# The block products of an f32 attention kernel as four products of 32 output rows, in column tiles

## The chip, the cores and the metric

One core of a Trainium2 chip. TensorE multiplies matrices and writes its results to PSUM (eight banks of 128 partitions by 512 f32 numbers); VectorE, ScalarE and GpSimd (POOL in the profile) read, add and copy; SyncE (SP) issues most of the DMAs between SBUF and memory. Each engine works through its own instructions in order, and engines wait for one another through semaphores. The metric is the time of one execution on the device, in microseconds (us).

## The reference

An input `x` of 8 batches, 512 positions and 512 features goes through attention with 16 heads of 32 features, whose queries and keys are conditioned by one vector a batch, and the result is added to `x`. All is float32. Without the reshaping into heads:

```python
Q, K, V = x @ Wq.T + bq, x @ Wk.T + bk, x @ Wv.T + bv
cQ = Q + (cond @ Wq.T + bq)
cK = K + (cond @ Wk.T + bk)
scores = cQ @ cK.T / sqrt(32)          # per batch and head
out = x + softmax(scores) @ V
```

## The kernel before, in words

Four heads make a group of 128 features, so there are 32 pairs of a batch and a head group, numbered `t` (`T = B * G`). The main loop goes over `t`, and each turn has four stages, `kc` from 0 to 3. In each stage TensorE does three things one after the other.

First come the scores of group `t` for 128 keys (`exponentials`, lines 565 to 584). Four matmuls with three rows each (L570, bf16) put the negated maxima of the queries into four PSUM banks, and four matmuls with 32 rows each (L573) add the scores. ScalarE turns the four banks into exponentials (L584).

Second come the row scores of group `t + 1` or `t + 2`, for 128 queries (`row_max`, `row_scores`, L499). They are used only for the maxima and the denominators: VectorE takes the maximum of each row (L490 for two banks, L508 for the other two together), and ScalarE takes the exponentials against it and adds them up (`denominators`, L518; each is followed by an instruction that reads the sum).

Third comes one of two things. In one stage of four it is the weighted sum of the group before (`weighted`, `times_v`, L589): four heads side by side, each with 32 columns of weights and its own 32 of the 128 output partitions, with 512 columns moving, and between them the sums' spreading (`spread_sums`, L620). VectorE then turns the result (L645), GpSimd divides and adds the residual (L646, L647), and SP stores it. In the other three stages it is a part of the projections of the next batch to queries, keys and values.

A projection of a pair of head groups is not computed as eight products of blocks but as seven, after Strassen and Winograd. The sums and differences of blocks of the weights (`combine_w`) and of the turned input (`combine_x`) are made ahead, and `product` (lines 397 to 406) multiplies one block by one block: 256 features are summed in two matmuls of 128 rows (`kc`), with 128 columns of weights held still and 256 columns moving, into half a bank. For queries and keys the block of the weights is still and the block of the input moves (L406); for the values it is the other way round (L403). `first_products` and `other_products` call it, seven matmuls' worth in each stage: the first does products 1, 6, half of 2, and 7; the other does 4, 5, the other half of 2, and 3. ScalarE copies product 1 away (L438), and VectorE adds the others up (L444 and L445 or L458 and L459, and `plus`, L426 or L429), reading the banks. The halves of a product are in the same order for every stage.

The order of all instructions on TensorE, ScalarE, VectorE and GpSimd is written out by hand (`tc.manual_schedule`). Which of the eight banks a stage uses for what is in the table `TURNS`, of which `banks` reads a row; the same pattern returns after two groups, that is eight stages. The maxima are split in three bf16 parts (`split_max`) and, in the main loop, turned by a DMA (`turn_max`), not by TensorE.

In the profile an f32 matmul of the program shows as two records on TensorE, each a weight load (engine PEld) and a pass (PE); a bf16 matmul shows as one. A stage with block products has 14 such records on lines 403 or 406.

Of the kernel before, what the change touches and what calls it, by code (L numbers as in the profile page):

```python
# [17 lines left out]
def kernel(  # L18
# [38 lines left out]
    nc = tc.nc  # L57
    P = 128
    B, S, D = x.shape
    HD = 32  # L60
    H = D // HD
    G = D // P
    HG = P // HD
# [5 lines left out]
    HS = S // 2  # L69
# [175 lines left out]
    for i in range(NS):  # L245
        r = slice(i * BL, (i + 1) * BL)
# [130 lines left out]
    def block_of_w(n, i, u, kc):  # L377
        f = MADE_OF[i - 1][0]
        if n == "v":
            at = slice(0, HS) if f != "22" else slice(HS, D)  # L380
            if isinstance(f, int):
                return wc[n][:, f, kc, :]
        else:
            g = u * 2 + (f == "22")
            at = slice(g * P, (g + 1) * P)
            if isinstance(f, int):
                return wc[n][:, f, kc, u * P : (u + 1) * P]
        return wT[n][:, kc + 2 * (f != "11"), at]

    def block_of_x(b, i, kc, at):  # L390
        f = MADE_OF[i - 1][1]
        if isinstance(f, int):
            return xc[:, f, kc, at]
        off = HS * (f == "22")
        return xT[b][:, kc + 2 * (f != "11"), at.start + off : at.stop + off]

    def product(n, b, u, i, pt, kcs=(0, 1)):

        for kc in kcs:
            w = block_of_w(n, i, u, kc)  # L400
            if n == "v":
                xb = block_of_x(b, i, kc, slice(u * P, (u + 1) * P))
                nc.tensor.matmul(pt, xb, w, start=(kc == kcs[0]), stop=(kc == kcs[-1]))  # L403
            else:
                xb = block_of_x(b, i, kc, slice(0, HS))
                nc.tensor.matmul(pt, w, xb, start=(kc == kcs[0]), stop=(kc == kcs[-1]))  # L406

    def twice(a):
        return a.unsqueeze(1).broadcast_to([P, 2, HS])
# [21 lines left out]
    def first_products(n, b, u, dens, small, at, first=0):  # L431


        one_, two_ = banks(first), banks(at)
        c1, c12, c2, c22 = parts_of(n, b, u)
        m1 = c2[:, 0, :]
        product(n, b, u, 1, one_[:, :HS])
        nc.scalar.copy(m1, one_[:, :HS])  # L438
        dens()
        product(n, b, u, 6, two_[:, :HS])  # L440
        small()
        product(n, b, u, 2, two_[:, HS:], (0,))
        product(n, b, u, 7, one_[:, HS:])
        nc.vector.tensor_tensor(c12, two_[:, :HS], m1, ALU.add)  # L444
        nc.vector.tensor_tensor(c1[:, 0, :], two_[:, HS:], m1, ALU.add)  # L445
        plus(n, b, u, 1, c22, one_[:, HS:], c12)
# [359 lines left out]
    for t in range(T - 3):  # L806
        b, r = divmod(t, G)
# [199 lines left out]
    b, g = divmod(t, G)  # L1007
# [55 lines left out]
```

## Time and profile before

| What | Value |
|---|---|
| median of 3 runs | 722.1 us (721.99 to 722.43) |
| the profiled execution | 722.59 us, of which the span is 720.8 us |
| TensorE passes busy | 714.2 us, 99% |
| TensorE weight loads busy | 401.3 us, 56% |
| VectorE busy | 528.0 us, 73% |
| ScalarE busy | 617.3 us, 86% |
| GpSimd busy | 176.3 us, 24% |
| DMA | 32.91 MB, mean 46 GB/s |

The span runs from the first instruction of the program to the last; the time of the execution has a little more around it. Busy time is the union of an engine's instructions, without the waits. Weight loads (PEld) overlap the passes (PE). In a row of a group or a chain, `L406` is line 406 of the kernel, `128*128 128x256` says that weights of 128 rows and 128 columns are held still and 256 columns move past 128 rows, and `x14` counts records. A row of busy times by stage has the stretch in us, its length, and then busy us and records of PE, PEld, VectorE (DVE), ScalarE (ACT) and POOL, the granted share of the TensorE clock, the DMA engines' mean busy share and the GB/s. In square brackets after a record stands how long its engine had been idle and what ended that. Where the text below gives start times with three decimals, they are those of single records of the trace, from the span's start.

### The profile page before, as it was taken

What the parts mean: (1) busy time and instruction counts of PE and PEld (TensorE: products, weight loads), DVE (VectorE), ACT (ScalarE), POOL (GpSimd) and SP (SyncE); (2) the same over time, 40 slices, a digit from 0 to 9 for tenths busy, and PEclk for the clock granted to TensorE, in tenths of its full rate; (3) what the DMA queues carried; (4) which work ended last, traced back from release to release, by engine and by line L of the source; (5) the groups of instructions that cost most, each with busy time, mean ns of one, the idle gap of its engine ahead of it and who ended that gap; (6) DMA issues with size and microseconds to landing.
All of it is one profiled execution on the core that took longest, in us unless ns stands there. A gap on an engine that the chain in (4) does not pass through costs nothing.

```text
span 720.8 us, 14892 instructions
## 1 busy us (share of the span) xinstructions
PE 714.2 (99%) x5296; PEld 401.3 (56%) x5296; DVE 528.0 (73%) x834; ACT 617.3 (86%) x1539; POOL 176.3 (24%) x275
## 2 busy tenths in 40 slices
PE   9999999999999999999999999999999999999997
PEld 7566555565555566555565555565555565555532
DVE  4798777777768777677776877777767767767777
ACT  2589989999899998989999889998989989889674
POOL 3712221122221122221122221122221122221351
PEclk9999999999999999999999999999999999999999
DMA  6733321222322222321322321323201222211211
GB/s 177 110 60 62 53 41 30 49 44 46 53 35 36 50 41 49 53 41 28 51 41 49 52 40 27 53 37 52 38 16 23 38 38 38 37 21 19 37 32 29
DMA packets 223358, 32.91 MB, mean 46 GB/s; under 512 B 221610, under 2 KB 222122, under 8 KB 223284
## 3 DMA queue, kind: packets, MB, share of 16 engines
q1 hardware_dynamic: 221524, 30.92, 25.3%
q10 hardware_dynamic: 1760, 1.05, 0.5%
q8 instruction: 41, 0.67, 0.4%
q14 instruction: 33, 0.27, 0.1%
HBM read 19.75 MB, written 8.39 MB: 39 GB/s over the span
## 4 chain that ended last, share of the span: by engine, by line
PE 97%; DVE 2%; issue 1%; DMA 1%; DVEq 0%
PE psum L406 27%; PE psum L499 16%; PE psum L589 15%; PE psum L403 14%; PE psum L573 14%; PE psum L570 5%; PE psum L350 2%; DVE acc L863 1%; PE psum L889 1%; DMA w_q<-in_L_cond_Wq_dram 1%; PE psum L266 0%; DVE acc L861 0%; PE psum L311 0%; PE psum L667 0%; PE psum L599 0%
## 5 line engine op out<-in xcount | busy, mean ns | idle before, releaser
L518 ACT ACTIVATE dead<-psum,nmax 128x512 f32<-128x512 f32 x480 | 327.6, 702 | 5.1 <-DVE nmax L490 3.1
L584 ACT ACTIVATE e<-psum 128x512 f32<-128x512 f32 x488 | 252.0, 602 | 64.2 <-PE psum L573 63.9
L490 DVE TENSOR_REDUCE nmax<-psum 128x1 f32<-128x512 f32 x240 | 154.5, 686 | 143.1 <-PE psum L499 143.1
L508 DVE TENSOR_REDUCE nmax<-psum 128x2 f32<-128x1024 f32 x130 | 157.7, 1214 | 2.8 <-PE psum L499 2.7
L499 PE MATMUL psum<-kT,qT 32*128 32x512 f32 x1024 | 143.9, 605 | 0.0
L646 POOL TENSOR_TENSOR res<-res,recs 128x512 f32<-128x512 f32 x30 | 31.5, 1049 | 432.1 <-DVE res L645 432.1
L573 PE MATMUL psum<-qT,kT 32*128 32x512 f32 x976 | 125.5, 587 | 0.0
L589 PE MATMUL psum<-e,v 128*32 128x512 f32 x1024 | 121.2, 596 | 0.0
L518 ACT ACTIVATION_READ_ACCUMULATOR dead<-psum,nmax 128x1 f32 x480 | 105.2, 219 | 0.0
L499 PEld LDWEIGHTS psum<-kT,qT 32*128 32x128 f32 x1024 | 59.8, 183 | 58.1 <-ACT dead L518 26.4
L589 PEld LDWEIGHTS psum<-e,v 128*32 128x32 f32 x1024 | 26.6, 110 | 65.1 <-issue 37.6
L573 PEld LDWEIGHTS psum<-qT,kT 32*128 32x128 f32 x976 | 48.6, 185 | 2.2
L403 PE MATMUL psum<-wc_v,xc 128*128 128x256 f32 x192 | 49.3, 379 | 0.0
L570 PE MATMUL psum<-maxT,onesb 3*128 3x512 bf16 x488 | 48.1, 384 | 0.0
L406 PE MATMUL psum<-xc,wc_k 128*128 128x256 f32 x180 | 46.2, 379 | 0.0
L406 PE MATMUL psum<-xc,wc_q 128*128 128x256 f32 x180 | 46.2, 379 | 0.0
L570 PEld LDWEIGHTS <-onesb 3*128 3x128 bf16 x488 | 12.3, 90 | 57.2 <-issue 57.2
L173 POOL TENSOR_TENSOR xr<-xr,bvs 128x512 f32<-128x512 f32 x31 | 39.4, 1272 | 18.7 <-DMA x<-in_x_dram 12.0
L403 PEld LDWEIGHTS psum<-wc_v,xc 128*128 128x128 f32 x192 | 36.5, 190 | 5.0
L647 POOL TENSOR_TENSOR res<-res,xr 128x512 f32<-128x512 f32 x30 | 38.2, 1273 | 2.4
L403 PE MATMUL psum<-wT_v,xT 128*128 128x256 f32 x128 | 37.1, 392 | 0.0
L406 PEld LDWEIGHTS psum<-xc,wc_k 128*128 128x128 f32 x180 | 34.2, 190 | 4.7
(165 smaller groups left out, 791.2 us busy)
## 6 DMA issues: line engine op xcount, KB each, us to landing
xr<-in_x_dram SPq DMA_DIRECT2D x124, 64.0 KB, 2.4
out_dram<-res SPq DMA_DIRECT2D x122, 64.0 KB, 1.9
x<-in_x_dram SPq DMA_DIRECT2D x112, 64.0 KB, 2.4
w_q<-in_L_cond_Wq_dram SPq DMA_DIRECT2D x4, 256.0 KB, 4.4
w_v<-in_L_cond_Wv_dram SPq DMA_DIRECT2D x16, 64.0 KB, 2.4
w_k<-in_L_cond_Wk_dram SPq DMA_DIRECT2D x16, 48.0 KB, 2.3
x<-in_x_dram ACTq DMA_DIRECT2D x2, 256.0 KB, 3.9
x<-in_x_dram SPq DMA_DIRECT2D x2, 256.0 KB, 4.2
```

What stands on the lines that cost most here:

```text
L173: nc.gpsimd.tensor_tensor(xr[t], xr[t], bias, ALU.add)
L403: nc.tensor.matmul(pt, xb, w, start=(kc == kcs[0]), stop=(kc == kcs[-1]))
L406: nc.tensor.matmul(pt, w, xb, start=(kc == kcs[0]), stop=(kc == kcs[-1]))
L490: nc.vector.tensor_reduce(nmax[t][:, qc, j : j + 1, 0], banks(HG + j), AX.X, ALU.max, negate=True)
L499: nc.tensor.matmul(pt, qkT["q", t][r, qc * P : (qc + 1) * P], qkT["k", t][r, :], start=True, stop=True,)
L508: nc.vector.tensor_reduce(nmax[t][:, qc, pr * 2 : pr * 2 + 2, 0], pt, AX.X, ALU.max, negate=True)
L518: nc.scalar.activation(dead, banks(HG + j), AF.Exp, bias=nmax[t][:, qc, j, :], accum_out=sums[t][:, qc, j, :],)
L570: nc.tensor.matmul(bank[j], onesb[r, :], maxT[t][r, :], start=True, stop=False)
L573: nc.tensor.matmul(bank[j], qkT["k", t][r, kc * P : (kc + 1) * P], qkT["q", t][r, :], start=False, stop=True,)
L584: nc.scalar.activation(e[:, i, :], bank[pr * 2 + i], AF.Exp)
L589: nc.tensor.matmul(pt[j * HD : (j + 1) * HD, :], vs[b % 2][:, kc, (g * HG + j) * HD : (g * HG + j + 1) * HD], es[t, kc, j // 2][:, j % 2, ...
L647: nc.gpsimd.tensor_tensor(y, y, xr.pop(t), ALU.add)
```

## The change

`product` splits every block matmul in four. Each of the four holds 32 of the 128 columns of the still block and writes the 32 output partitions that belong to them, in a column tile of its own; all four read the same moving block. This is the form that the weighted sum (L589) has, with 256 columns moving instead of 512. The two cases (values, queries and keys) now share one matmul line.

```diff
         for kc in kcs:
             w = block_of_w(n, i, u, kc)
             if n == "v":
-                xb = block_of_x(b, i, kc, slice(u * P, (u + 1) * P))
-                nc.tensor.matmul(pt, xb, w, start=(kc == kcs[0]), stop=(kc == kcs[-1]))
+                still, moving = block_of_x(b, i, kc, slice(u * P, (u + 1) * P)), w
             else:
-                xb = block_of_x(b, i, kc, slice(0, HS))
-                nc.tensor.matmul(pt, w, xb, start=(kc == kcs[0]), stop=(kc == kcs[-1]))
+                still, moving = w, block_of_x(b, i, kc, slice(0, HS))
+            for j in range(HG):
+                r = slice(j * HD, (j + 1) * HD)
+                nc.tensor.matmul(
+                    pt[r], still[:, r], moving, start=(kc == kcs[0]), stop=(kc == kcs[-1])
+                )
```

`HG` is 4 and `HD` is 32. Nothing else is changed: the blocks, the banks, the order of the stages and the work of the other engines are as before.

## The prediction

> **What bounds the kernel now.** The page's busy line, the clock row and the chain that ended last come first.
>
> ```profile
> PE 714.2 (99%) x5296; PEld 401.3 (56%) x5296; DVE 528.0 (73%) x834; ACT 617.3 (86%) x1539; POOL 176.3 (24%) x275
> PEclk9999999999999999999999999999999999999999
> ...
> PE 97%; DVE 2%; issue 1%; DMA 1%; DVEq 0%
> ```
>
> TensorE bounds nearly the whole span, at full clock. But ScalarE is busy 86%, so a gain on TensorE may soon meet it. The chain in order of time shows what a stage is made of (start, us, line, records):
>
> ```profile
> 305.39 0.33 PE psum L570 x4
> 305.71 0.86 PE psum L573 x8
> 306.57 0.94 PE psum L499 x8
> 307.51 3.22 PE psum L406 x14
> 310.73 0.33 PE psum L570 x4
> 311.06 0.86 PE psum L573 x8
> 311.92 0.86 PE psum L499 x8
> 312.78 0.99 PE psum L589 x8
> 313.77 0.05 PE psum L620 x7
> 313.82 2.59 PE psum L589 x24
> ```
>
> Every stage is exponentials' scores (L570, L573), row scores (L499), then either block products (L403/L406, seven products of two matmuls) or the weighted sum (L589). An f32 matmul is two records, each a weight load and a pass. So a stream of products is 14 records, 3.22 us; the trace has 92 such streams, 1288 records. The change touches only these. The weighted sum already has the form that the products get: four tiles of 32 columns side by side, with 512 columns moving instead of 256. The durations of the records in these two stages:
>
> ```profile
> L406 PEld LDWEIGHTS psum<-xc,wT_q x4: 186/190/190, 307.4 to 308.0; 128*128 128x128 f32 x4
> L406 PE MATMUL psum<-xc,wT_q x4: 379/379/483, 307.4 to 308.2; 128*128 128x256 f32 x4
> ...
> L589 PEld LDWEIGHTS psum<-e,v x32: 106/110/113, 312.7 to 315.4; 128*32 128x32 f32 x32
> L589 PE MATMUL psum<-e,v x32: 592/592/617, 312.7 to 315.8; 128*32 128x512 f32 x32
> ```
>
> Read record by record, a product stream starts with a load at 307.444 and matmuls at 307.445, 307.765, then every 216 ns. The first step is 320 because the first load (107 ns up to the next load's start) lies in the open. The last record starts at 310.355 and the next stage's load at 310.663: 308 ns of exit. 320 + 12x216 + 308 = 3220, the 3.22 of the chain. All 92 streams have these steps. In the weighted sum four records start 7 ns apart, and a group follows the last after 429 to 430 ns (24 records, six groups, 2.59 us); its first step is 454.
>
> The busy times by stage show that TensorE is not alone in setting the length: the first two rows have the same kind of work, and so have the last two.
>
> ```profile
> 294.69:299.95 5.26, 5.26 (x38) 3.50 (x34) 3.82 (x6) 4.30 (x12) 2.81 (x5) 1.00 0.16 29
> 299.95:305.32 5.36, 5.36 (x35) 3.48 (x34) 3.66 (x7) 5.11 (x14) 1.97 (x4) 1.00 0.47 82
> ...
> 310.66:316.34 5.68, 5.68 (x61) 1.74 (x60) 5.01 (x9) 5.15 (x14) 0.00 (x0) 1.00 0.30 49
> ...
> 332.24:338.02 5.78, 5.78 (x61) 1.90 (x60) 5.07 (x10) 5.53 (x15) 0.00 (x0) 1.00 0.31 49
> ```
>
> The tenth between them is a late row score. The timeline of the weight loads names what they waited for:
>
> ```profile
> 306.38 0.30 PEld L499 LDWEIGHTS psum<-kT,qT 32*128 32x128 f32 x7 [0.22 <-ACT dead L518]
> ...
> 311.63 0.32 PEld L499 LDWEIGHTS psum<-kT,qT 32*128 32x128 f32 x8 [0.54 <-DVE qT L429]
> ```
>
> A row score needs a bank that ScalarE's last exponential of the stage before (L518) or VectorE's last sum of it still reads. A load released by 0.99 us after the stage's start costs nothing; at 306.38 it is at 1.07, and the stage is 83 ns longer.
>
> **The change, part by part.**
>
> *Removed:* 1288 full records: 92 streams of 320 + 12x216 + 308 = 3220 ns.
>
> *Added:* 5152 records of 32 columns with as many loads, 14 groups of four in a stream. The step between groups: 512 moving columns take 430 ns in four tiles and also 430 in one full matmul (project_qk's L350 records at 22.37 and 22.80), so tiles cost no streaming time; 256 columns then take the 216 that they take now. From below, half of 429 is 214.5, 20 ns less over a stream; from above, see the rivals (236 and 248). I take 216, since L589 is the nearest row. The four loads of a group are hidden under the group before, as in L589, if 216 ns hold them: at 313.59 four loads, then eight passes of 16 columns, start within 48 ns.
>
> ```profile
> 313.59 0.23 PE L620 MATMUL psum<-apart,modulo 128*32 128x16 f32 x8
> ```
>
> *Entry:* a load of 32 columns keeps the first pass waiting 28 ns (312.709 to 312.737) instead of 107. L589's first step is 24 ns over its later ones; here 216 + 24.5 = 240.5 against 320: 79.5 saved. *Exit:* the fourth tile starts 20 ns after the first (313.653, 313.673), so the stream ends 20 ns later. The turn between shapes itself costs the same: L499 to L406 516 ns, L499 to L589 515; last start to the L570 load 308, and 521 with 213 of it for the longer pass. A stream becomes 240.5 + 12x216 + 20 + 308 = 3160.5: 59.5 ns less, 92 times, 5.5 us if nothing else is late.
>
> *More instructions to fetch:* 7,728 records on TensorE's 10,592. The instruction queue moved 0.67 MB in 41 packets; it becomes some 1.2 MB, beside 32.9 MB of data on engines about a quarter busy. Nothing on the path, while fetching runs ahead. No wait, DMA or order on SP or POOL moves. ScalarE and VectorE read the same banks; beside column tiles (310.66 to 316.34) an L518 takes 677 to 719 ns, beside full products 687 to 718, so no slower readers: cost nothing.
>
> *What is late next.* The pattern of stages repeats every two head groups, 43.33 us: eight stages, six with products, 14 times from t = 1 on (84 of the 92 streams). I follow 59.5 ns through one round, by stage starts:
> - 294.69: its stream ends 59.5 earlier, but the row scores at 299.95 already wait 97 ns for ScalarE's last L518 of this stage, which started from L573 and is not earlier. Lost to the stall.
> - 299.95: L573 was earlier all the same, so ScalarE's chain is (it idles 0.25 us before L584, enough). The next stall keeps its 83. Gain kept.
> - 305.32: VectorE's last sum (L429) waits for the stream's end and follows it; ScalarE is done 0.76 us into the next stage, and 0.94 would do (a load follows it by 51 ns). Kept.
> - 310.66: weighted sum, untouched.
> - 316.34: L429 starts at 5447 ns of the stage, released by the stream's end; but the sum before it (L459, until 5491, which the next instruction overlaps by 82) would allow 5409. 38 ns kept, 21.5 lost as a longer wait at 321.63.
> - 321.63: kept. The next stage's loads move from 0.92 to 0.98 us, just inside.
> - 326.98: the next stage, 332.24, waits 103 ns for ScalarE. Lost.
> - 332.24: weighted sum.
>
> Kept: 3x59.5 + 38 = 216.5 of 357 ns a round, 0.50%; 14 rounds, 3.0 us. Of the eight early streams, between none and all of 0.48; half, 0.24. Sum 3.3 us. The profiled execution took 722.59 (span 720.8 and 1.8 around it); its span becomes 717.5, its time 719.3. It stood 0.5 over the median, 722.1, so the predicted median is 718.8.
>
> *Against a rule.* How fast can TensorE be fed? After a late bank, its sequencer's wait ends at 313.121; by 313.674, 31 loads and passes behind it have started, at most 18 ns each, and seven of them within 74 ns. A group of eight in 216 ns asks for 27. The Trainium skill (TensorE: Matmul & The Clock Gate, section "Wait — 56ns, not 53.3ns?") says that with hardware decoding off a matmul costs its sequencer about 62 ns, which binds once the array's work is shorter. By it a group of four would be an estimated 248 ns and the kernel near 749, by the row 718.8.
>
> **The rivals.**
>
> *The whole gain arrives.* If the late releases move with TensorE, all 92x59.5 = 5.5 us show: 716.6. For: ScalarE idles 0.25 to 0.96 us in each stage. Against: the stalls at 299.95 and 332.24 go back to an L573 a whole stage earlier.
>
> *Nothing arrives.* ScalarE or VectorE takes back the other 3 us too, or the step is 4 to 5 ns longer (13x4.6 = 59.5): 721 to 723. For: at 321.63 both are within 70 ns of late. Against: L429's wait on the stream's end in two of the six.
>
> *Slower: the array is not fed fast enough.* Place: the groups inside the 92 streams. Four small transposes, L707 at 7.42 to 7.62, come 62 ns apart, load and pass; four such pairs make 248 instead of 216. A stream then gains 13x32 and loses 59.5: +356.5, 92 times 32.8 us, less the 389 ns a round of present stalls that a later TensorE no longer meets (5.8): +27, 749. If instead the 20 ns between first and fourth tile are paid again in every group (236): +200.5 a stream, 18.4 - 5.8, +12.6, 735. It decides from about 223 ns a group. For: no row has four tiles with only 256 columns each. Against: the 18 ns above, and L707 loads 128 columns, L589 32; in L589 the 20 ns are not paid again.
>
> **How the numbers follow.** The forecast has 0.58, the whole gain 0.10, nothing 0.12, slower 0.20. This measurement can tell about 0.2%, 1.4 us. Faster is 0.58 + 0.10 = 0.68, same 0.12, slower 0.20. The forecast's own range is 716.9 to 720.6. The whole range goes from 716.0 (the whole gain, with half a us over) to 727: it takes in no change and a step of up to about 226 ns, and leaves out some 0.16 of the slower cases.
>
> **What would show it.** L403/L406 with loads of 110 ns, matmul starts 7 ns apart in fours, groups 216 apart, first step 240; streams in the chain at 3.16 us. Row scores at the stages that answer to 299.95 and 332.24 wait 60 ns more for L518; the round is 43.12 instead of 43.33. It is wrong if groups stand over 220 apart, if TensorE's idle time is put down to "issue" inside a stream, or if L518 and L429 hold the row scores in other stages.

## The result, and the profile after

The changed kernel takes 719.71 us (median of 7 runs, 719.44 to 720.93) against 722.1 for the kernel before: a ratio of 0.9968, with a 95% interval of 0.9957 to 0.9979. The prediction was 718.8. The profiled execution took 719.44 us, its span 717.7. The code lines moved by three: L403 and L406 are now L407, and L499, L573, L589, L518 and L429 are L502, L576, L592, L521 and L432.

The page's busy line, clock row and chain that ended last:

```profile
PE 710.9 (99%) x9160; PEld 321.6 (45%) x9160; DVE 527.1 (73%) x834; ACT 617.4 (86%) x1539; POOL 176.4 (25%) x275
PEclk9999999999999999999999999999999999999999
...
PE 95%; DVE 2%; DMA 1%; issue 1%; POOL 0%; SPq 0%; DVEq 0%; POOLq 0%
```

TensorE has 1.7 times the records and 3 us less busy time; its loads are busy 80 us less. DMAs have 1% of the chain, as before; but now the page's chain by line names the DMA that turns the maxima among them, which it did not before. The chain in order of time, for the two stages that answer to those shown before (the first has query products, the second the weighted sum):

```profile
303.61 0.33 PE psum L573 x4
303.94 0.86 PE psum L576 x8
304.80 0.97 PE psum L502 x8
305.77 3.16 PE psum L407 x56
308.93 0.33 PE psum L573 x4
309.25 0.86 PE psum L576 x8
310.11 0.89 PE psum L502 x8
311.00 0.99 PE psum L592 x8
311.99 0.05 PE psum L623 x7
312.04 2.59 PE psum L592 x24
```

A stream of products is 3.16 us instead of 3.22, within 2 ns of what was predicted: over all 92 streams the first step is 240 ns, the others 215 to 216, the fourth tile starts 20 ns after the first, and in 88 of the 92 the exit to the next stage's first pass is the same 311 or 312 ns as before. But the row scores (L502) in the two stages have grown from 0.94 to 0.97 and from 0.86 to 0.89: part of the gain is spent there. The durations of the records:

```profile
L407 PEld LDWEIGHTS psum<-xc,wT_q x16: 106/110/110, 305.7 to 306.2; 128*32 128x32 f32 x16
L407 PE MATMUL psum<-xc,wT_q x16: 379/379/403, 305.7 to 306.4; 128*32 128x256 f32 x16
```

The busy times by stage, for the same four stages of a round as before (the first two and the last two have the same kind of work):

```profile
292.98:298.19 5.20, 5.20 (x80) 2.63 (x76) 3.78 (x6) 4.19 (x12) 2.82 (x4) 1.00 0.10 18
298.19:303.54 5.36, 5.36 (x80) 2.66 (x76) 3.66 (x7) 5.16 (x14) 1.96 (x4) 1.00 0.55 95
...
308.85:314.56 5.71, 5.71 (x64) 1.72 (x60) 5.06 (x9) 5.21 (x15) 0.00 (x0) 1.00 0.29 46
...
330.30:336.13 5.84, 5.84 (x64) 1.94 (x60) 5.16 (x10) 5.64 (x15) 0.00 (x0) 1.00 0.31 49
```

The first stage is 60 ns shorter; the second is as long as before, and the last 54 ns longer: there nearly the whole 60 ns came back as a wait. What the row scores' loads waited for:

```profile
304.63 0.30 PEld L502 LDWEIGHTS psum<-kT,qT 32*128 32x128 f32 x7 [0.24 <-ACT dead L521]
...
309.86 0.31 PEld L502 LDWEIGHTS psum<-kT,qT 32*128 32x128 f32 x8 [0.57 <-DVE qT L432]
```

The same releasers as before. These loads start 1.09 and 1.00 us after the first record of their stages (303.54, 308.86), where it was 1.07 and 0.97.

For the rest, "a round" is eight stages, and its length the sum over the eight of the median stage in 13 or 14 rounds (of the mean in the fifth, which alternates between two values). In ns, by the starts in the round shown of before:

| Stage | work | before | predicted | after |
|---|---|---|---|---|
| 294.69 | keys | 5264 | 5205 | 5205 |
| 299.95 | values | 5360 | 5360 | 5355 |
| 305.32 | queries | 5346 | 5286 | 5314 |
| 310.66 | weighted sum | 5680 | 5680 | 5705 |
| 316.34 | keys | 5273 | 5213 | 5209 |
| 321.63 | values | 5351 | 5313 | 5322 |
| 326.98 | queries | 5264 | 5205 | 5204 |
| 332.24 | weighted sum | 5782 | 5842 | 5836 |
| sum | | 43320 | 43104 | 43150 |

A round is 170 ns shorter, not 216. Fourteen rounds made 2.3 of the 3.15 us between the two spans; the stretch before the first main stage made 0.72 (four streams there, 0.24; for the rest see the runs' starts below), the stretch up to the steady rounds 0.13, and the tail nothing.

### The profile page after: what moved, and what is told of

Same layout as the page of the kernel before. It is cut to its first block, busy times and chain, and to the rows that moved or that the text cites. A ratio compares the mean times of both kernels' runs of the same rounds, so it can differ in the third digit from the quotient of the medians.

```text
span 717.7 us, 22620 instructions
## 1 busy us (share of the span) xinstructions
PE 710.9 (99%) x9160; PEld 321.6 (45%) x9160; DVE 527.1 (73%) x834; ACT 617.4 (86%) x1539; POOL 176.4 (25%) x275
## 4 chain that ended last, share of the span: by engine, by line
PE 95%; DVE 2%; DMA 1%; issue 1%; POOL 0%; SPq 0%; DVEq 0%; POOLq 0%
PE psum L407 40%; PE psum L502 17%; PE psum L592 15%; PE psum L576 14%; PE psum L573 5%; PE psum L350 2%; DVE acc L866 1%; DMA x<-in_x_dram 1%; PE psum L892 1%; DMA maxT<-split 1%; DVE acc L864 0%; PE psum L670 0%; PE psum L602 0%; PE psum L266 0%; SPq L653 0%
## 5 line engine op out<-in xcount | busy, mean ns | idle before, releaser
L521 ACT ACTIVATE dead<-psum,nmax 128x512 f32<-128x512 f32 x480 | 327.8, 707 | 5.6 <-DVE nmax L493 3.1
L493 DVE TENSOR_REDUCE nmax<-psum 128x1 f32<-128x512 f32 x240 | 154.6, 686 | 140.9 <-PE psum L502 140.9
L511 DVE TENSOR_REDUCE nmax<-psum 128x2 f32<-128x1024 f32 x130 | 157.8, 1215 | 2.7 <-PE psum L502 2.7
L502 PE MATMUL psum<-kT,qT 32*128 32x512 f32 x1024 | 146.5, 608 | 0.0
L576 PE MATMUL psum<-qT,kT 32*128 32x512 f32 x976 | 125.4, 587 | 0.0
L592 PE MATMUL psum<-e,v 128*32 128x512 f32 x1024 | 121.2, 596 | 0.0
L521 ACT ACTIVATION_READ_ACCUMULATOR dead<-psum,nmax 128x1 f32 x480 | 107.7, 224 | 0.0
L502 PEld LDWEIGHTS psum<-kT,qT 32*128 32x128 f32 x1024 | 60.2, 183 | 60.6 <-ACT dead L521 23.1
L592 PEld LDWEIGHTS psum<-e,v 128*32 128x32 f32 x1024 | 26.6, 110 | 65.1 <-issue 37.6
L407 PE MATMUL psum<-wc_v,xc 128*32 128x256 f32 x768 | 50.2, 379 | 0.0
L576 PEld LDWEIGHTS psum<-qT,kT 32*128 32x128 f32 x976 | 48.5, 185 | 2.2
L573 PE MATMUL psum<-maxT,onesb 3*128 3x512 bf16 x488 | 48.1, 385 | 0.1
L407 PE MATMUL psum<-xc,wc_q 128*32 128x256 f32 x720 | 47.1, 379 | 0.0
L407 PE MATMUL psum<-xc,wc_k 128*32 128x256 f32 x720 | 47.1, 379 | 0.0
L573 PEld LDWEIGHTS <-onesb 3*128 3x128 bf16 x488 | 12.2, 91 | 64.5 <-issue 62.3
L407 PE MATMUL psum<-wT_v,xT 128*32 128x256 f32 x512 | 36.8, 382 | 0.0
L407 PE MATMUL psum<-xT,wT_q 128*32 128x256 f32 x480 | 34.5, 382 | 0.0
L407 PE MATMUL psum<-xT,wT_k 128*32 128x256 f32 x480 | 34.5, 382 | 0.0
```

The costliest lines, as they stand in the source:

```text
L407: nc.tensor.matmul(pt[r], still[:, r], moving, start=(kc == kcs[0]), stop=(kc == kcs[-1]))
L493: nc.vector.tensor_reduce(nmax[t][:, qc, j : j + 1, 0], banks(HG + j), AX.X, ALU.max, negate=True)
L502: nc.tensor.matmul(pt, qkT["q", t][r, qc * P : (qc + 1) * P], qkT["k", t][r, :], start=True, stop=True,)
L511: nc.vector.tensor_reduce(nmax[t][:, qc, pr * 2 : pr * 2 + 2, 0], pt, AX.X, ALU.max, negate=True)
L521: nc.scalar.activation(dead, banks(HG + j), AF.Exp, bias=nmax[t][:, qc, j, :], accum_out=sums[t][:, qc, j, :],)
L573: nc.tensor.matmul(bank[j], onesb[r, :], maxT[t][r, :], start=True, stop=False)
```

## The experiments

The theory after the result: the tiles save 59.5 ns in each stream, by the shorter first load less the stagger of the tiles, and ScalarE's last exponential of a stage and VectorE's last sum take a part of it back, because the next row scores need their banks. The rivals: the saving comes from column tiles as such; what is missing is lost for another reason; TensorE is fed too slowly.

**Two tiles of 64 columns.**

```diff
-            for j in range(HG):
-                r = slice(j * HD, (j + 1) * HD)
+            for j in range(2):
+                r = slice(j * 2 * HD, (j + 1) * 2 * HD)
```

> The changed kernel with two tiles of 64 columns instead of four of 32. Theory (the saving is the first weight load of a stream, which is proportional to its columns, less the stagger between first and last tile): the load keeps the first pass waiting 54 ns, the first step is 267 (240 with four tiles, 320 with one), the last tile starts 7 ns after the first, the steps stay 216; a stream is 3174 ns, between 3162 and 3222. Whether VectorE and ScalarE hear of a product's end 31 ns later after its last record, as with four tiles, or 10 or 0, tells whether that delay belongs to column tiles as such. Time about 720. Rival (the saving comes from column tiles as such, such as a cheaper turn from row tiles): the first step is 240 again.

Measured: first step 266 to 267 ns, later steps 216, second tile 6 to 7 ns after the first; a stream 3175 ns. Time 719.55 us, ratio 0.9969 (0.9957 to 0.9982). The loads by form, then the chain in order of time:

```profile
L407 PEld LDWEIGHTS psum<-xc,wc_q 128*64 128x64 f32 x360 | 25.9, 137 | 13.0
```

```profile
306.99 3.17 PE psum L407 x28
```

A load takes 110, 137 or 190 ns for 32, 64 or 128 columns, and the first step 240, 267 or 320. The differences are the same, so the saving is the first load, and column tiles as such bring nothing. The updates of semaphores in the traces tell one thing more. The release of TensorE's semaphore, from which ScalarE and VectorE learn that a product is done, comes 392 to 393 ns after the start of the last record with full products, 402 to 403 with two tiles, 423 to 424 with four: the delay grows with the tiles. This explains why two tiles lose nothing: their stream is 13 ns longer, but VectorE starts earlier after it, and the round is 43149 ns, as with four. The wait for VectorE follows the release in the same way: the sum that holds the row scores of the fourth stage of the table (L429, later L432) ends 911, 922 and 943 ns into that stage with one, two and four tiles. The Trainium skill (TensorE: Matmul & The Clock Gate, section "The cost: per-tile semaphore tail") has such a tail and gives it 4.7 ns for each further tile with one increment; here it is some 10.

**ScalarE's copy of product 1 moved to VectorE**, in the changed kernel and in the kernel before. Three stages of a round have this copy (L438 before, L441 after), and it is in these that ScalarE ends late.

```diff
-        nc.scalar.copy(m1, one_[:, :HS])
+        nc.vector.tensor_copy(m1, one_[:, :HS])
```

> The changed kernel (tiles of 32 columns), with the copy of product 1 moved from ScalarE to VectorE; three stages of the eight in a round have that copy, some 0.40 us of ScalarE each. Theory (ScalarE's last exponential of those stages ends late, makes the next row scores wait, and so eats part of what the tiles save): the waits of 149, 108 and 156 ns in a round of the changed kernel fall to 0, about 30 and 0; a round becomes about 42.77 us instead of 43.15, the time about 714.4 us. Rival (the row scores wait for something else, VectorE's sums or the banks): VectorE now has 0.37 us more in these stages, the waits stay or grow, and the time is 719.7 or more.

> The kernel before (full products), with the same copy moved from ScalarE to VectorE. Theory: its waits of 97, 83 and 103 ns in a round go, a round becomes 43.03 us instead of 43.31, the time about 718.1 us. Between this and the tiled kernel with the same copy the round then differs by some 0.26 us, against 0.17 between the two kernels with the copy on ScalarE: most of what was eaten comes back. Rival (what the tiles save is lost for another reason than ScalarE): the difference between the two stays 0.17 a round.

Measured: 749.8 us (ratio 1.0395) and 754.27 (1.0449). Both forecasts of the time failed, though the waits went where the theory said: the row scores of the three stages that follow a copy take 438 or 439 ns in both kernels, from the start of their first record to that of the last, which is what they take where nothing holds them up. A new wait took their place. The chain of the tiled one, in a stage with key products:

```profile
308.23 1.05 DVE nmax L493 x2
309.28 0.14 issue
309.41 1.21 DVE nmax L511
310.63 0.34 DVE kT L441
310.97 0.04 issue
311.01 1.07 PE psum L407 x16
```

On VectorE the copy stands behind the row maxima (L493, L511), and product 7, which writes the other half of the bank that the copy reads, waits for the copy (L441). In each of the three stages the stream is 0.74 to 0.81 us longer. The expectation counted VectorE's queue, and not who waits for the bank.

**The copy left out**, again in both kernels, so that nothing takes its place; product 1 is then computed but missing from the result.

```diff
-        m1 = c2[:, 0, :]
+        m1 = wT[n][:, 0, :HS]
         product(n, b, u, 1, one_[:, :HS])
-        nc.scalar.copy(m1, one_[:, :HS])
```

> The changed kernel without ScalarE's copy of product 1: the sums that used the copy add a block of the weights instead, so product 1 is computed and left out of the result. Unlike the copy on VectorE, nothing is put behind it in VectorE's queue and product 7 need not wait for it. Theory (ScalarE's late end ate the gain): the row scores of the three stages after a copy take 438 ns like the undisturbed ones instead of 587, 546 and 594, the others stay as they are; a round is 42.73 us instead of 43.16, the time about 713.8 us. Rival (VectorE's sums or the banks would hold the row scores next): they stay over 500 somewhere among the three, and the round is over 42.9.

> The kernel before (full products) without the same copy, product 1 left out of the result in the same way. Theory: row scores of 438 ns in the three stages instead of 534, 519 and 540, a round of 43.04 us instead of 43.32, the time about 718.1 us. The tiles are then worth 0.30 us a round, 4.3 us in all, where with the copy they are worth 0.17 and 2.4. Rival (what is lost of the tiles' 59.5 ns a stream has nothing to do with ScalarE): the tiles are still worth 0.17 a round.

Measured: 715.69 us with tiles (ratio 0.9913, 0.9898 to 0.9928) and 719.47 with full products (0.9966, 0.9953 to 0.9979). The rounds are 42775 and 43042 ns: the tiles are worth 267 ns a round here, and 170 with the copy. In the full kernel all three row scores are down to 438 or 439; in the tiled one two are, and the one of the third stage, 546 before, is 478. The busy times by stage in the tiled one, the first three stages and the last of a round, and then the second, third and last of the full one:

```profile
291.32:296.53 5.21, 5.21 (x80) 2.64 (x76) 3.78 (x6) 4.35 (x11) 2.83 (x4) 1.00 0.09 17
296.53:301.73 5.21, 5.21 (x80) 2.65 (x76) 3.58 (x7) 4.78 (x13) 1.96 (x4) 1.00 0.51 89
301.73:306.98 5.25, 5.25 (x80) 2.62 (x76) 3.63 (x7) 4.93 (x13) 0.00 (x0) 1.00 0.19 30
...
328.42:334.10 5.68, 5.68 (x64) 1.94 (x61) 4.74 (x9) 5.30 (x15) 0.00 (x0) 1.00 0.30 49
```

```profile
298.25:303.51 5.26, 5.26 (x35) 3.55 (x34) 3.60 (x7) 4.78 (x13) 1.95 (x4) 1.00 0.56 95
303.51:308.77 5.26, 5.26 (x35) 3.50 (x34) 3.62 (x7) 4.89 (x14) 0.00 (x0) 1.00 0.05 8
...
330.35:336.03 5.68, 5.68 (x61) 1.99 (x60) 4.71 (x9) 5.24 (x15) 0.00 (x0) 1.00 0.31 49
```

The stages that took 5.36, 5.31 and 5.84 with tiles take 5.21, 5.25 and 5.68, and those that took 5.36, 5.35 and 5.78 with full products take 5.26, 5.26 and 5.68. Of the 357 ns a round that six streams save, late releases took 187 with the copy and take 90 without it. So it is shown that ScalarE's late end, as the copy makes it, took about half; the rival that nothing would come back is out. Of the 90, some 40 are in the third stage, where the trace still names ScalarE's exponential. The other 53 are in the fourth and sixth stage of the table, whose row scores wait as long as with the copy (462 and 553 ns). There VectorE's last sum ends some 943 ns into the stage, with the copy or without, and 912 with full products; that this sum is the cause is read from these times, and no run took it away.

The times came out 1.9 us (tiles) and 1.4 us (full) over what was expected. Three stages in each profiled execution are 0.18 to 0.34 us longer than their like (0.92 and 0.85 us in all). In the tiled one the stage at 553.17 is one of them, 0.34 us longer: its next scores waited for the DMA of the last experiment. In the full one the stage at 249.62 stands behind a VectorE transposition that started 0.36 us late with no releaser named. And there were 2.3 us around these spans, not 1.8. The rest stays open.

**One part alone: queries and keys, or values.** The diff is that of queries and keys; the other has `n != "v"`.

```diff
+            if n == "v":
+                nc.tensor.matmul(pt, still, moving, start=(kc == kcs[0]), stop=(kc == kcs[-1]))
+                continue
             for j in range(HG):
```

> Four tiles for the products of queries and keys (four of the six streams of a round), full products for the values. By the path through a round: the first key stream's gain is lost in the wait for ScalarE, and this time also for the stage after it, since its full stream starts no earlier; the first query stream keeps 36 of 60, as VectorE hears of the end 31 ns later; the second key stream keeps about 30; the second query stream is lost but for some 6. A round is 72 ns shorter than 43.32, the time 721.1 us. Rival (each stream keeps the same share of its 60): four sixths of 165, 110 ns a round, 720.5 us.

> Four tiles for the products of the values (two of the six streams of a round), full products for queries and keys. By the path: the first value stream keeps about 30 of 60 (ScalarE's copy of product 1 comes 30 earlier, since the signal of its end is 31 ns later), the second keeps all but a few ns. A round is 87 ns shorter than 43.32, the time 720.9 us. Rival (each stream keeps the same share): two sixths of 165, 55 ns a round, 721.3 us.

Measured: the round with tiles for queries and keys is 43252 ns, 68 shorter (72 by the path, 110 by equal shares), with tiles for the values 43217, 103 shorter (87 and 55). Two of the six streams bring more than the other four, as the path through the stages has it; the value streams bring 16 ns more than I gave them. The two parts add up to 171 ns, the 170 of the whole change. The times decide less: 722.07 us for queries and keys (ratio 1.0000, 0.9990 to 1.0009; expected 721.1) and 721.0 for values (0.9992, 0.9983 to 1.0002; expected 720.9). The start scatters more than this effect: TensorE's first product record stands between 28.9 and 31.0 us in the profiled executions of these kernels, which are alike up to there, and the latest is the one with tiles for queries and keys, which was also the longest of its ten executions (721.07 to 723.19).

**128 moving columns instead of 256.**

```diff
-        for kc in kcs:
+        for at in (slice(0, P), slice(P, HS)):
+            for kc in kcs:
...
-                    pt[r], still[:, r], moving, start=(kc == kcs[0]), stop=(kc == kcs[-1])
+                        pt[r, at],
+                        still[:, r],
+                        moving[..., at],
...
```

> The changed kernel with each of its matmuls split once more, 128 moving columns instead of 256: 28 groups of four in a stream, eight records in the time of 128 columns. Theory (TensorE is fed at 18 ns an instruction or faster): a group takes between 109 and 144 ns, a stream 3.2 to 4.2 us, the time between 722 and 815. Rival (it is fed at 62 ns for a load and a pass): 248 a group, a stream near 7 us, the time over 1000 us; then the 216 of the changed kernel would have had to be slower as well, which it isn't, unless instructions pile up ahead of a stream.

Measured: groups of four 109 ns apart, a stream of 112 records in 3197 ns, 726.56 us (one run). The chain shows a stream; the timeline of the loads shows a later stage's start:

```profile
308.59 3.19 PE psum L408 x112
```

```profile
415.96 0.10 PEld L578 LDWEIGHTS <-onesb 3*128 3x128 bf16 x4 [1.51 <-DMA maxT<-split]
```

Eight loads and passes in 109 ns are 13.6 ns each, sustained over a stream of 224: TensorE can be fed about twice as fast as the changed kernel asks (27), and the slower rival is out at its root. The 62 ns for a matmul that the Trainium skill gives for hardware decoding off (TensorE: Matmul & The Clock Gate, section "Wait — 56ns, not 53.3ns?"), which the prediction weighed, would make an estimated 248 of these 109; they don't hold in these runs. Still the kernel is 7.1 us slower in its span than the changed one. Its rounds are only some 0.12 us longer (1.6 us); 5.3 us are nine stages of values after which the next scores waited for a DMA, up to 1.3 us each; in each of the nine a packet of instructions for TensorE started 1.9 to 2.6 us after this DMA's issue. That led to the last experiment.

**What makes the DMA late.** In the main loop a DMA turns the maxima (L544 before, L547 after). It stands in the third stage of a turn in the program; by the trace it is issued in the fourth, the values (at 300.1 in the stage from 298.19 on, for one), and the stage after that needs it at its start. For the DMA's tile the trace says, in the kernel before:

```profile
L544 SPq DMA_TRANSPOSE maxT<-split x29: 1188/1188/2249, 62.3 to 668.9; - x29
...
DMA to landing us min/median/max: 2.4/2.5/2.8
```

and in the changed kernel, with the engine that waited (us, times):

```profile
L547 SPq DMA_TRANSPOSE maxT<-split x29: 1188/1189/1301, 61.5 to 665.9; - x29
...
  PEld L573: 2.2, 5
...
DMA to landing us min/median/max: 2.4/2.5/4.1
```

The trace gives a landing for 18 of the 29. None is over 2.8 us before, four are over 3.8 in the changed kernel, and nine over 3.6 with 128 moving columns. The instruction queue that grows with TensorE's records (q8) has 41, 72 and 112 packets. Of these thirteen late DMAs, twelve had a packet of this queue start while they were under way or just before. The thirteenth, issued at 558.8 in the changed kernel, had none; a packet of the other instruction queue (q14) started 2.0 us after its issue. To test it, 30 more of the small matmuls that fill TensorE's first microseconds:

```diff
-    for _ in range(28):
+    for _ in range(58):
         nc.tensor.matmul(warm[:, :P], onesb, onesb, start=True, stop=True)
```

> The changed kernel with 30 more of the small matmuls that fill TensorE's first microseconds (58 instead of 28): 60 instructions more ahead of all others, and nothing else; they cost some 1.7 to 3.2 us at the start. In the changed kernel four of the DMAs that turn the maxima landed after 3.8 to 4.1 us, where 2.4 is usual: the ones issued at 191, 364, 536 and 559 us. Theory (they land late because a fetch of instructions for TensorE, one in about 256 of its instructions, falls into their flight): 60 instructions more move every fetch some 2.2 us against the work, so these four land in time (2.4 to 2.7 us) and others are late: of those whose landing the trace shows, the ones of the changed kernel's 83, 170, 256, 342, 408, 428, 515, 580 and 601 us. Rival (they are late for another cause, such as the stores and loads of those stages, which recur at the same places): the same four are late again.

```profile
  PEld L573: 2.1, 4
...
DMA to landing us min/median/max: 2.4/2.9/4.7
```

Measured: the four that were late now land in 2.4 to 2.6 us. Of the nine expected late, eight are (3.4 to 4.7 us); the one issued at 408 is not (2.5), and one at 300 that was not expected is somewhat late (3.1), with no packet of q8 in its flight. A fetch of TensorE's instructions under way makes this DMA late; that is shown, not only argued. When the fetch starts matters. Over the traces of all eleven kernels, 24 of these DMAs had one start 0.2 to 2.1 us after their issue, and all 24 landed after 3.1 to 4.4 us. Of 17 in which it started later still, 13 landed in 2.4 to 2.8 us and four in 4.5 to 4.7. Of 5 in which it started up to 0.1 us before the issue, four landed in 3.6 to 3.7. Of 152 with no such start from 0.2 us before the issue to the landing, 149 landed in 2.4 to 2.8 us. The time, 721.19 us, contains the matmuls at the start.

No run gave a version that beats the changed kernel with the whole computation in it; two tiles equal it, with 51 instruction packets instead of 72.

## Why the prediction was right

- *The stream.* Predicted 3160.5 ns (240.5, twelve steps of 216, 20, 308), measured 3162. Taking the weighted sum's records as the row for the new form was right, down to the stagger. (One of the 92 streams of before has a first step of 272 ns, not 320; nothing rests on it.)
- *The turn between shapes* costs what it did: 311 or 312 ns at the exit and 517 at the entry, before and after.
- *Feeding TensorE.* The 18 ns a record read behind one late bank was an upper bound; with 128 moving columns it is 13.6.
- *Part of the gain is eaten by late releases.* The path through the round had the right stages: at 294.69 and 326.98 the gain was lost to ScalarE, and at 316.34 and 321.63 half and all of the stream's gain were kept (30 of 60 lost in the next wait, where 21.5 were predicted). The copy left out shows the cause for the waits on ScalarE.
- *What was mis-sized.* 216 ns were to be kept a round, 170 were. The failing terms are "ScalarE's chain is (earlier)" at 299.95 and "VectorE's last sum (L429) waits for the stream's end and follows it" at 305.32. The first looked at L573 alone and left out that the copy in this chain waits for product 1; the second took the end of a stream, as VectorE learns of it, to move with TensorE's own end. It doesn't: the release comes 423 ns after the last record's start instead of 392. The copy starts 23 to 24 ns after the release of product 1 in the kernel before, with two tiles and with four. So at 299.95 it came some 34 ns earlier and not 59.5 (its stage starts 59 ns earlier, and it starts 25 ns later in the stage), and the wait at 305.32 grew by 27. L432 ended some 32 ns later against the next stage, which put the row scores at 310.66 over the limit, from 439 to 463 ns: a sign of being wrong that the prediction had named (row scores held in another stage) came true there, on a small scale. The row was in the trace of before: the release after L589's last record comes 636 ns after its start, which is 423 and the 213 ns for twice the columns. I had read it for TensorE's turn and not for the signal.
- *Fetching more instructions, "nothing on the path".* In the changed kernel this held for TensorE's fetches: the three DMAs that they are seen to make late (issued at 191.1, 363.7 and 536.4) landed at 195.25, 367.70 and 540.42, some 0.4 us before the next scores began, and these stages are no longer than their like. One stage at 557.1 is 189 ns longer, its next scores waiting for the DMA issued at 558.8; that one had no fetch of TensorE's under way, so this cost is not shown to come from the added records. "No wait, DMA or order moves" was too strong all the same: with twice the records the waits for this DMA cost 5.3 us.
- *A rival's price.* 389 ns a round in 14 rounds are 5.4 us; the other 0.4 of the 5.8 has no source in the sum, so the slower rival's 749 and 735 may stand that much too low.
- *The median* was missed by 0.9 us, while the span came within 0.2: the start of that one execution was 0.7 us earlier than in the one before, of which the four streams there explain 0.24. The rounds gave 2.3 us, not 3.0, and a start that was earlier by more than the tiles explain made up for it: that the span came so close is luck.

## What to carry to other kernels

Where TensorE goes from one stage's shape to another, the first weight load of a stage lies in the open, here nearly in proportion to its columns; tiles of fewer columns shorten it, and here cost nothing in streaming, though the matmul fills the array (216 ns a step with one, two and four tiles). Before counting such a gain, follow it through the stages that repeat: who releases each bank next, and whether that engine's chain starts early enough to move along. And count the signal of an end separately from the end itself: here four tiles shortened the stream by 60 ns and the news of its products by only 30.

## What was not expected of the hardware

A fetch of TensorE's instructions (72 packets for the changed kernel's 18,320 records on TensorE, one for some 254) that starts 0.2 to 2.1 us after the issue of the DMA that turns 128 x 512 bf16 numbers made it land after 3.1 to 4.4 us instead of 2.4 to 2.8, in 24 of 24 cases. Whether a fetch for another engine does the same is open: two late DMAs (3.8 us in the changed kernel, 3.7 with the copy left out) had a packet of q14 and none of q8 start 2.0 us after their issue. And the release of a semaphore after the last record comes some 10 ns later for each further column tile: 392 ns with one, 402 with two, 423 with four.
